# A Mamba-and-ConvLSTM kernel: fold matmuls queued before fills, a later table phase, and paired projection tiles

## The chip, the cores and the metric

The kernel runs on one core of a Trainium2 chip. The time is device microseconds of that core, from one launch; the median of three runs is given. Five engines run their own instruction streams in order and wait for each other through semaphores: TensorE (PE in the profile; PEld is its weight load), VectorE (DVE), ScalarE (ACT), GpSimd (POOL) and SyncE (SP, which issues the DMAs).

## What is computed

The input is `(1, 64, 256, 128)`: 64 channels, T = 256 times, F = 128 frequencies. Layer 0 is a bidirectional Mamba block, first along time (128 sequences of length 256), then along frequency (256 sequences of length 128). Layer 1 is a convolutional LSTM over 32 windows of 8 times. In short:

```python
def _mamba(u, p):
    x, z = split(einsum('nld,ed->nle', u, p['in_proj_w']), 2)
    x = silu(depthwise_conv(x, p['conv_w'], width 4, causal) + p['conv_b'])
    dt, Bm, Cm = split(einsum('nld,ed->nle', x, p['x_proj_w']), [4, 20])
    dt = softplus(dt @ p['dt_proj_w'].T + p['dt_proj_b'])
    def step(h, inp):                       # h: 128 channels x 16 states
        dA = exp(dt_t * A)
        h = dA * h + dt_t * B_t * x_t
        return h, einsum('nds,ns->nd', h, C_t)
    y = scan(step) + x * p['Dp']
    return einsum('nld,od->nlo', y * silu(z), p['out_proj_w'])

def _block(u, p):   return _mamba(_rmsnorm(u, p['norm_w']), p) + u
def _bimamba(u):    return concat([_block(u, pf), flip(_block(flip(u), pb))])
# time stage, then frequency stage:  x = x + _bimamba(x) @ lin_w + lin_b
# layer 1: global norm, unfold, ConvLSTM over 32 windows, transposed conv, prelu, residual
```

All of it is float32.

## The kernel before, in words

`Stage` is run twice, stage 0 along time and stage 1 along frequency. Each cuts its 32,768 positions into 64 chunks of 512. A chunk takes 16 slots: two directions d, two state halves q, four blocks b of 32 channels. Slot S of the loop in `run` handles one (d, q, b) with all 512 positions of two states at once, on tiles of 128 x 1024.

A slot's chain goes over four engines:

- `inputs` ("the fill", line 555): 32 small matmuls of 64 x 32 tiles put dt\*B\*x into one of two `bx` buffers in PSUM. It reads `dtxT` (the transposed dt\*x) and `D` (B spread on a mask by DVE, line 444).
- `decays` (line 575): two ACT exponentials make dA in one of four buffers from `rep`, which a DMA brings from DRAM with each row repeated. Every first use of a buffer in a direction also clears one column (line 572).
- `recur` (line 583): one DVE scan, h = dA\*h + bx, into one of seven `h` buffers (`NH`).
- `outputs` (line 589): POOL multiplies h by `C`, also spread by a DMA.
- every fourth slot, `add_up` ("the fold", line 598): eight matmuls of 128 x 32 tiles add four h tiles into the one bank `y`. Only then are those four h buffers free.

After eight slots DVE's `gate` (line 614) makes `yz` = y\*silu(z); after sixteen, `close_a` and `close_b` (lines 623 to 629) put both directions through the output projection and the residual into `po`, and `keep` (lines 639 and 647) writes X.

The order of the work is written out by hand. In slot S the engines are given: the scan of S, the gate, POOL's product of S-1, the fill of S+2, the decays of S+2, the fold, and then what the table `HEAD` has for this slot. `HEAD` names each preparing step of a chunk with the slot, counted from the start of the chunk before it, at which it is queued. Negative slots lie a further chunk ahead. Each engine runs its share strictly in that order.

The steps of `HEAD` for one chunk, in the order in which data passes through them: `load` u by DMA; `squares`, `means`, `rms` (ACT, TensorE, ACT); `normalise` (POOL writes `xn`, then four DMAs on SP, line 309, copy it into `unp` twice, shifted by one); `project_x` (lines 328 and 329) and `project_z` (line 332) on TensorE, each copied out by ACT to `xs` and `zs`; `silus` (line 353 loads ACT's table, 357); `step_sizes` (pv, line 363); `softplus` (377, 373, and 380 loads the exponential's table again); `project_bc` (line 407, ACT copy line 409, then four DMAs `away<-bc`, line 416); `dt_away` (DMA `there<-dt`, line 386); `times_x` (POOL, line 397); `spread_dt` and `spread_c` (DMAs `rep<-there`, line 459, and `C<-away`, line 453, 512 KB each); `turn` (TensorE transposes, lines 429 and 431, ACT copy 433); `diagonal` (DVE, line 444). "The table phase" is `silus` to `softplus`: three table loads with the silus and the softplus between them, on ACT.

All DMAs stand in SP's one queue, in program order. The tiles `pm`, `px`, `pz`, `pv`, `pb`, `pt` and `po` share two PSUM buffers (`mm`).

Layer 1 (`ConvLstm`, from about 7190 us on) and the start of each stage (`first`) are touched only in that `first` calls the changed helpers.

Of the kernel before, what the change touches and what calls it, by code (L numbers as in the profile page):

```python
# [29 lines left out]
F32 = mybir.dt.float32  # L30
BF16 = mybir.dt.bfloat16
AF = mybir.ActivationFunctionType
# [4 lines left out]
P = 128  # L37
C = 64
T = 256
F = 128  # L40
NS = 16
NBC = 2 * NS
# [3 lines left out]
NU = 4  # L46
W = 64
RANK = 4
NTOK = 512
# [8 lines left out]
FH = F // 2  # L58
HALF = T // 2
NRING = 4  # L60
NREP = 3
RESPOND = 6
NH = 7
LAG = 2
EXP_AND_LN = "natural_log_exp_and_others"
# [5 lines left out]

HEAD = (
    (-13, "load"),
    (-11, "squares"),
    (-6, "means"),
    (-6, "rms"),
    (-5, "normalise"),
    (-2, "project_x", 0),
    (-1, "project_z", 0),
    (-1, "project_z", 1),  # L80
    (0, "project_x", 1),
    (4, "silus"),
    (4, "step_sizes"),
    (5, "softplus"),
    (6, "project_bc", 0),
    (6, "dt_away", 0),
    (6.5, "dt_away", 1),
    (7, "times_x", 0),
    (8.5, "spread_dt", 0, 0),
    (9, "spread_c", 0, 0),  # L90
    (10, "turn", 0),
    (11, "diagonal", 0, 0, 0),
    (12, "spread_dt", 0, 1),
    (12, "project_bc", 1),
    (12.5, "times_x", 1),
    (13, "diagonal", 0, 0, 1),
    (13.5, "spread_c", 0, 1),
    (15, "diagonal", 0, 1, 0),
    (17, "diagonal", 0, 1, 1),
    (17.5, "spread_dt", 1, 0),  # L100
    (17.5, "spread_c", 1, 0),
    (18, "turn", 1),
    (19, "diagonal", 1, 0, 0),
# [3 lines left out]
    (23, "diagonal", 1, 1, 0),  # L107
    (25, "diagonal", 1, 1, 1),
)
SECOND = tuple(x for x in HEAD if x[0] >= 12 and x[1] != "project_bc")  # L110


class Mamba:
# [3 lines left out]
    def __init__(self, ctx, tc, cols, room, d):  # L117
        nc = tc.nc
        self.nc, self.tc, self.d, self.cols = nc, tc, d, cols
        cp = ctx.enter_context(tc.tile_pool(name="m_const", bufs=1))  # L120
# [9 lines left out]
        for i in range(4):  # L130
            for n, t, rows, width in (
                ("g1", self.G1, P, P),
                ("g2", self.G2, P, P),
                ("wz", self.Wz, C, P),
                ("wdt", self.Wdt, P, P),
                ("w2", self.W2, P, C),
            ):
                t.append(cp.tile([rows, width], F32, name=f"{n}{i}", tag=f"{n}{i}"))
        for i in range(2):
            self.W3.append(cp.tile([P, 2, C], F32, name=f"w3{i}", tag=f"w3{i}"))  # L140
        b = cp.tile([C, 2], F32, name="lin_b")
        self.b = b
        self.lin_b = [b[:, i : i + 1] for i in range(2)]

        room = room.rearrange("p t f -> p (t f)")
        at = 0
# [16 lines left out]
        for h in range(2):  # L163
            own = slice(h * C, (h + 1) * C)
# [6 lines left out]
    def load(self, first):  # L171
        dma, d = self.nc.sync.dma_start, self.d
        if first:
            dma(out=self.win[:, 0], in_=d["in_proj"][:, 0])
            dma(out=self.cw[:, 0], in_=d["conv_w"][0].partition_broadcast(C))
            dma(out=self.cols, in_=d["cols"])
            dma(out=self.xdt, in_=d["dt_proj"])
            dma(out=self.Wbc, in_=d["x_proj_bc"])
        else:
            dma(out=self.win[:, 1:4], in_=d["in_proj"][:, 1:4])  # L180
            dma(out=self.cw[:, 1:4], in_=d["conv_w"][1:4].partition_broadcast(C))
            dma(out=self.lin, in_=d["lin_w"])
            dma(out=self.b, in_=d["lin_b"])
            dma(out=self.ow, in_=d["out_proj"])

    def shifts(self, i):
# [15 lines left out]
        self.nc.vector.tensor_copy(self.Wdt[i], ps[:, 0:P])  # L202

    def gates(self, i):
        self.nc.vector.tensor_copy(self.Wz[i], self.win[:, i, P : 2 * P])

    def masks(self):

# [16 lines left out]
class Stage:  # L225
# [102 lines left out]
        nc.tensor.matmul(self.seqs(px), lhsT=m.G1[i], rhs=self.unp[:, :, first : first + L], start=True, stop=False)  # L328
        nc.tensor.matmul(self.seqs(px), lhsT=m.G2[i], rhs=self.unp[:, :, second : second + L], start=False, stop=True)  # L329

    def gated(self, pz, i):
        self.nc.tensor.matmul(  # L332
            self.seqs(pz), lhsT=self.m.Wz[i], rhs=self.unp[0:C, :, 3 : 3 + self.L], start=True, stop=True
        )

    def project_x(self, ch, d):
        i = 2 * self.stage + d
# [3 lines left out]
        self.nc.scalar.activation(xs, px, AF.Identity, bias=self.m.cb[:, i : i + 1])  # L341
        self.at["xs", ch, d] = xs

    def project_z(self, ch, d):
        pz = self.mm("pz")
        self.gated(pz, 2 * self.stage + d)
        zs = self.wk.tile([P, NTOK], F32, name="zs", tag="zs", bufs=5)
        self.nc.scalar.copy(zs, pz)
        self.at["zs", ch, d] = zs

    def silus(self, ch):
        nc = self.nc
# [48 lines left out]
        )  # L401
        self.at["dtx", d] = dtx

    def project_bc(self, ch, d):

        pb = self.mm("pb")[0:NBC]
        self.nc.tensor.matmul(pb, lhsT=self.m.Wbc[:, 2 * self.stage + d], rhs=self.at["xs", ch, d], start=True, stop=True)  # L407
        t = self.wk.tile([NBC, NTOK], F32, name="bc", tag="bc")
        self.nc.scalar.copy(  # L409
            self.in_turns(t, "p (u i c) -> p i u c"), self.in_turns(pb, "p (i u c) -> p i u c")  # L410
        )
        away = self.dram.tile([NS // 2, 2, 2, NTOK // 2], F32, name="away", tag="away")
        for g in range(2):
            rows = self.in_turns(t[NS + NS // 2 * g : NS + NS // 2 * (g + 1)], "p (u i c) -> p i u c")
            for i in range(2):
                self.nc.sync.dma_start(
                    out=away[:, i, g].rearrange("a (u c) -> a u c", u=NU), in_=rows[:, i]
                )
        self.at["bc", d], self.at["away", ch, d] = t, away

    def turn(self, ch, d):

        nc, m = self.nc, self.m
        dtx, bc = self.at["dtx", d], self.at["bc", d]
        pt = self.mm("pt")
        bt = self.ps_bt.tile([P, NU, NS], F32, name="bt", tag="bt")
        for u in range(NU):
            own = slice(P * u, P * (u + 1))
            nc.tensor.transpose(pt[:, own], dtx[:, own], m.ident)  # L429
        for u in range(NU):  # L430
            nc.tensor.transpose(bt[:, u], bc[0:NS, P * u : P * (u + 1)], m.ident[0:NS, 0:NS])  # L431
        t = self.wk.tile([P, NU, P], F32, name="dtxT", tag="dtxT", bufs=2)
        nc.scalar.copy(t.rearrange("p u d -> p (u d)"), pt)  # L433
        self.at["dtxT", ch, d], self.at["bt", ch, d] = t, bt
# [35 lines left out]
    def first(self):  # L470


        nc, m = self.nc, self.m
        s, time = 2 * self.stage, self.time
        banks = [self.ps_bx.tile([P, 2, NTOK], F32, name="bx", tag="bx") for _ in range(2)]
# [14 lines left out]
        x, z = {}, {}  # L490
# [23 lines left out]
            m.gates(1)  # L514
            m.dt(1, self.mm("pw"))
        self.shifted(banks[0][:, 1], s + 1)
        for d in range(2):
            self.gated(banks[1][:, d], s + d)
        nc.scalar.preload_act_table_set(SILU)
        nc.scalar.activation(x[1], banks[0][:, 1], AF.Silu, bias=m.cb[:, s + 1 : s + 2])  # L520
        for d in range(2):
# [94 lines left out]

    def close_a(self, ch):
        nc, m = self.nc, self.m  # L620
        u, w3 = self.at["u", ch], m.W3[self.stage]
        self.po = po = self.mm("po")
        nc.tensor.matmul(po[0:C], lhsT=m.W2[2 * self.stage], rhs=self.at["yz", 0], start=True, stop=False)  # L623
        n = NTOK // 2
        for h in range(2):
            nc.tensor.matmul(po[0:C, h * n : (h + 1) * n], lhsT=w3[:, h], rhs=u, start=False, stop=False)

    def close_b(self, ch):
        self.nc.tensor.matmul(  # L629
            self.po[0:C], lhsT=self.m.W2[2 * self.stage + 1], rhs=self.at["yz", 1], start=False, stop=True  # L630
        )

    def keep(self, ch):
        nc, nseq, po = self.nc, self.nseq, self.po
        bias = self.m.lin_b[self.stage]
        if self.time:
            res = po[0:C].rearrange("p (f h t) -> p h t f", f=nseq, h=2)
            for h in range(2):
                nc.scalar.activation(
                    self.X[h * C : (h + 1) * C, :, ch * nseq : (ch + 1) * nseq], res[:, h], AF.Identity, bias=bias  # L640
                )
        else:
            res = po[0:C].rearrange("p (h r f q) -> p q r h f", h=2, f=FH, q=2)
            rows = slice(ch * nseq // 2, (ch + 1) * nseq // 2)
            for q in range(2):
                own = slice(q * C, (q + 1) * C)
                nc.scalar.activation(  # L647
                    self.X[own, rows, :].rearrange("p r (h f) -> p r h f", h=2),
                    res[:, q],
                    AF.Identity,  # L650
                    bias=bias,
                    accum_out=self.moments.sums[own, ch : ch + 1],
                )

    def spread_of(self, ch):

# [7 lines left out]
    def run(self):  # L664
        nch = NCH
        last = 16 * nch
# [6 lines left out]
        for S in range(int(min(steps)), last + LAG + 4):  # L673
# [3 lines left out]
                self.gate(*self.where(S - 8)[:2])  # L677
            if 0 < S <= last:
                self.outputs(S - 1)
            if 0 <= S + 2 < last:  # L680
                self.inputs(S + 2)

            for ahead in ((2, 3) if S % 16 == silu else () if S % 16 == silu + 1 else (2,)):
                if 0 <= S + ahead < last:
                    self.decays(S + ahead)
            if S % 4 == 1 and 4 < S <= last + LAG:
                self.add_up(S - LAG)
            for f, args in steps.get(S, []):
                f(*args)
            if S % 8 == LAG and 0 < S < last:  # L690
                self.skip(*self.where(S)[:2])
            if S % 16 == LAG and S > 16:
                self.close_a(S // 16 - 1)
            if S % 16 == LAG + 1 and S > 16:
                self.close_b(S // 16 - 1)
                self.keep(S // 16 - 1)
            for f, args in steps.get(S + 0.5, []):
                f(*args)
            if not self.time and S > 16:
# [5 lines left out]
                n = S // 16 - 1  # L705
                if S % 16 == RESPOND:
                    if 0 < n < 21:
# [533 lines left out]
```

## Time and profile before

| what | value |
|---|---|
| time, median of 3 runs | 7876.34 us (7869.36 to 7904.41) |
| the profiled execution: time, span | 7882.31 us, 7880.5 us |
| mean granted TensorE clock | 0.91 of full |
| scans: number, first and last start | 2048, at 46.7 and 7185.4 us |
| busy, share of the span: PE, DVE, ACT, POOL | 81%, 81%, 62%, 71% |
| DMA: moved, mean rate | 695.10 MB, 88 GB/s |

In the profile, a line of a group names the code line, the engine, the operation, output and input tiles with their shapes, the count, and then the busy time, the mean of one in ns, and the idle time of that engine just before with what ended most of it. In a timeline a line has start and length in us. A matmul in float32 shows as two records, so that `px` with its two matmuls is four records. Engines overlap; the shares of busy time are means over the whole span, while a chunk of 16 slots repeats 128 times and takes about 55 us of it.

### The profile page before, as it was taken

To read this page: it belongs to the slowest core of one execution; us is meant where nothing else is said; L and a number is where in the kernel's file an instruction comes from. 1 tells how busy PE (TensorE), PEld (TensorE's weight loads), DVE (VectorE), ACT (ScalarE), POOL (GpSimd) and SP (SyncE) were. 2 spreads that over 40 slices of the span, in tenths; PEclk is the share of its full clock that TensorE was granted. 3 is DMA by queue.
4 is the path that set the end of the run, shared out by engine and by line. 5 is a ranking of instruction groups with operands and counts; after the bars stand their busy time and mean duration, and the time that the engine had idled before them with its cause. 6 is when DMAs were issued, how large, how long until landed. Compare 5 with 4: busy or idle time off the path is not lost.

```text
span 7880.5 us, 324564 instructions
## 1 busy us (share of the span) xinstructions
PE 6410.5 (81%) x148488; PEld 3602.5 (46%) x148488; DVE 6363.7 (81%) x4166; ACT 4921.4 (62%) x8918; POOL 5571.1 (71%) x2898
## 2 busy tenths in 40 slices
PE   7878788888878787877888888877878777877999
PEld 3444444444444444443444444444444444445887
DVE  6888888888888888876888787888878888886887
ACT  6666666666666666665666666666666666664333
POOL 5777777777777777775777777777777777775554
PEclk8889999988899898988999898999889899998999
DMA  2222222222222222222323222222222222221000
GB/s 91 96 94 98 97 97 95 97 95 94 96 95 97 94 98 94 98 92 72 101 98 102 95 100 95 96 94 94 94 91 96 92 98 93 94 96 64 13 16 17
DMA packets 301986, 695.10 MB, mean 88 GB/s; under 512 B 72772, under 2 KB 129732, under 8 KB 300616
## 3 DMA queue, kind: packets, MB, share of 16 engines
q1 hardware_dynamic: 300616, 674.33, 25.3%
q8 instruction: 1166, 19.10, 1.1%
q14 instruction: 204, 1.67, 0.1%
HBM read 557.25 MB, written 83.89 MB: 81 GB/s over the span
## 4 chain that ended last, share of the span: by engine, by line
PE 33%; DVE 9%; ACT 5%; issue 4%; DMA 1%; POOL 1%; SPq 0%; DVEq 0%; POOLq 0%; ACTq 0%
PE bx L555 9%; DVE h L583 7%; PE cv L1003 6%; PE y L598 5%; PE pv L363 3%; ACT dA L575 2%; DVE D L444 2%; PE px L328 2%; PE pz L332 2%; PE px L329 1%; ACT L353 1%; ACT X L647 1%; PE po L629 1%; PE po L623 1%; POOL h L589 1%
## 5 line engine op out<-in xcount | busy, mean ns | idle before, releaser
L589 POOL TENSOR_TENSOR h<-h,C 128x1024 f32<-128x1024 f32 x2048 | 4824.4, 2371 | 1456.4 <-DVE h L583 1324.6
L583 DVE TENSOR_TENSOR_SCAN h<-dA,bx 128x1024 f32<-128x1024 f32 x2048 | 4614.8, 2275 | 1018.8 <-PE y L598 812.6
L555 PE MATMUL bx<-D,dtxT 64*32 64x128 f32 x131072 | 2578.3, 292 | 880.1 <-DVE h L583 872.5
L555 PEld LDWEIGHTS bx<-D,dtxT 64*32 64x32 f32 x131072 | 1994.9, 112 | 2351.7 <-DVE h L583 1007.3
L575 ACT ACTIVATE dA<-rep,cols 128x510 f32<-128x510 f32 (+1 forms) x4096 | 2657.0, 709 | 12.0 <-DVE h L583 6.0
L444 DVE TENSOR_TENSOR D<-mask,bt 128x1024 f32<-128x1024 f32 x1026 | 1226.0, 1195 | 9.7 <-PE bt L431 9.7
L598 PE MATMUL y<-h,fold 128*32 128x512 f32 x8192 | 1085.1, 648 | 6.0 <-POOL h L589 6.0
L363 PE MATMUL pv<-xs,wdt 128*128 128x512 f32 x512 | 452.2, 1035 | 510.3 <-ACT xs L357 508.8
L433 ACT COPY dtxT<-pt 128x512 f32<-128x512 f32 x256 | 150.0, 586 | 966.2 <-PE pt L429 966.1
L341 ACT ACTIVATE xs<-px,cols 128x512 f32<-128x512 f32 x252 | 173.6, 689 | 573.7 <-PE px L329 573.7
L409 ACT COPY bc<-pb 32x512 f32<-32x512 f32 x256 | 147.4, 576 | 518.7 <-PE pb L407 517.6
L598 PEld LDWEIGHTS y<-h,fold 128*32 128x32 f32 x8192 | 229.7, 118 | 520.5 <-issue 504.8
L397 POOL TENSOR_TENSOR dtx<-dt,xs 128x512 f32<-128x512 f32 x256 | 326.9, 1277 | 162.4 <-ACT dt L373 146.9
L363 PEld LDWEIGHTS pv<-xs,wdt 128*128 128x128 f32 x512 | 133.6, 286 | 666.6 <-ACT xs L357 595.9
L614 DVE TENSOR_TENSOR yz<-y,zs 128x512 f32<-128x512 f32 x256 | 176.9, 691 | 291.2 <-PE y L598 291.2
L407 PE MATMUL pb<-xs,wbc 128*32 128x512 f32 x512 | 311.9, 696 | 0.0
L328 PE MATMUL px<-unp,g 128*128 128x512 f32 x504 | 285.5, 648 | 22.1 <-DMA unp<-xn 20.5
L329 PE MATMUL px<-unp,g 128*128 128x512 f32 x504 | 259.1, 595 | 0.0
L332 PE MATMUL pz<-unp,wz 64*128 64x512 f32 x504 | 250.7, 616 | 0.0
L1126 POOL TENSOR_TENSOR y<-v,X 128x512 f32<-128x512 f32 x32 | 40.7, 1271 | 230.5 <-DVE v L1124 230.5
L572 ACT COPY dA<-zeros 128x4 f32<-128x4 f32 (+1 forms) x1024 | 194.9, 190 | 3.3 <-DVE h L583 3.2
L373 ACT ACTIVATE dt<-pv,cols 128x512 f32<-128x512 f32 x256 | 172.5, 687 | 25.3 <-issue 20.5
(191 smaller groups left out, 5458.1 us busy)
## 6 DMA issues: line engine op xcount, KB each, us to landing
rep<-there SPq DMA_DIRECT2D x512, 512.0 KB
C<-away SPq DMA_DIRECT2D x512, 512.0 KB
there<-dt SPq DMA_DIRECT2D x1024, 64.0 KB
unp<-xn SPq DMA_DIRECT2D x504, 64.0 KB
away<-bc SPq DMA_DIRECT2D x1024, 8.0 KB
u<-in_x SPq DMA_DIRECT2D x128, 64.0 KB
out<-y SPq DMA_DIRECT2D x32, 256.0 KB
w<-in_W_ih_f SPq DMA_DIRECT2D x10, 512.0 KB
```

Source lines behind the costliest of these rows:

```text
L328: nc.tensor.matmul(self.seqs(px), lhsT=m.G1[i], rhs=self.unp[:, :, first : first + L], start=True, stop=False)
L329: nc.tensor.matmul(self.seqs(px), lhsT=m.G2[i], rhs=self.unp[:, :, second : second + L], start=False, stop=True)
L332: self.nc.tensor.matmul(self.seqs(pz), lhsT=self.m.Wz[i], rhs=self.unp[0:C, :, 3 : 3 + self.L], start=True, stop=True)
L363: self.nc.tensor.matmul(pv, lhsT=self.m.Wdt[i], rhs=self.at["xs", ch, d], start=True, stop=True)
L397: self.nc.gpsimd.tensor_mul(self.in_turns(dtx, own), self.in_turns(self.at["dt", ch, d], natural), self.in_turns(self.at["xs", ch, d], nat ...
L444: self.nc.vector.tensor_mul(D, self.m.mask.unsqueeze(1).unsqueeze(1).to_broadcast([P, n, 2, W]), b.unsqueeze(3).to_broadcast([P, n, 2, W]),)
L555: self.nc.tensor.matmul(bx[DB * j : DB * (j + 1), i, :, u], lhsT=dtxT[rows, u, DB * b : DB * (b + 1)], rhs=D[rows, u, j], start=True, stop ...
L575: nc.scalar.activation(dA[:, :, g, :, live], rep[:, :, :, live], AF.Exp, scale=m.A[:, k, n : n + 1])
L583: self.nc.vector.tensor_tensor_scan(h[:, step], dA[:, step], bx[:, step], 0.0, ALU.mult, ALU.add)
L589: self.nc.gpsimd.tensor_mul(h, h, self.at["C", ch, d, q])
L598: nc.tensor.matmul(y[DB * b : DB * (b + 1)].rearrange("p (i t) -> p i t", i=2), lhsT=self.m.fold, rhs=hs[b][:, g], start=False, stop=q == ...
L1003: self.nc.tensor.matmul(t[:, g, :, 0:n_out], lhsT=wts[s][:, gate * P : (gate + 1) * P], rhs=self.parts[n][:, :, s : s + n_out], start=s == ...
```

## The change

Five things are done together.

1. In `run`, the fold (`add_up`) of a slot is queued ahead of the fill (`inputs`) and the decays, where it stood behind them.
2. `HEAD` is moved: `silus` and `step_sizes` from slot 4 to 6, `softplus` 5 to 7, `project_bc` of d=0 from 6 to 8, `dt_away` 6 and 6.5 to 8 and 8.5, `times_x` of d=0 7 to 8.5, `spread_dt` 8.5 to 9.5, `spread_c` 9 to 10.5, `squares` 5 to 8.5 (-11 to -7.5). `decays` runs one slot further ahead in the slot that has `silus`, so that dA of the next two slots (now 8 and 9) is queued ahead of the table phase. `RESPOND`, a small step of 20 chunks in stage 1, goes from slot 6 to 12.
3. `project_z` does both directions in one step. The weights of d=1 lie on rows 64 to 127 and are multiplied with the copy of xn on those rows, so that the two matmuls use different halves of TensorE's rows.
4. `project_bc` does both directions in slot 8: two matmuls into different 32-column groups, one ACT copy of 64 partitions, eight `away` DMAs. The step of d=1 in slot 12 is gone.
5. `close_a` and `close_b` become `close`, in slot 3 of the next chunk: each matmul of 512 positions becomes two of 256 that write different halves of `po`'s partitions. The residual's two of 256 become four of 128. `keep` is one ACT instruction over 128 partitions where it was two over 64.

```diff
-RESPOND = 6
+RESPOND = 12
 HEAD = (
-    (-11, "squares"),
+    (-7.5, "squares"),
...
-    (-1, "project_z", 0),
-    (-1, "project_z", 1),
+    (-1, "project_z"),
     (0, "project_x", 1),
-    (4, "silus"),
-    (4, "step_sizes"),
-    (5, "softplus"),
-    (6, "project_bc", 0),
-    (6, "dt_away", 0),
-    (6.5, "dt_away", 1),
-    (7, "times_x", 0),
-    (8.5, "spread_dt", 0, 0),
-    (9, "spread_c", 0, 0),
+    (6, "silus"),
+    (6, "step_sizes"),
+    (7, "softplus"),
+    (8, "project_bc", 0, 1),
+    (8, "dt_away", 0),
+    (8.5, "dt_away", 1),
+    (8.5, "times_x", 0),
+    (9.5, "spread_dt", 0, 0),
     (10, "turn", 0),
+    (10.5, "spread_c", 0, 0),
     (11, "diagonal", 0, 0, 0),
     (12, "spread_dt", 0, 1),
-    (12, "project_bc", 1),
...
-    (17.5, "spread_dt", 1, 0),
+    (17, "spread_dt", 1, 0),
...
+    def gated(self, pz):
+        for d in range(2):
+            rows = slice(d * C, (d + 1) * C)
+            self.nc.tensor.matmul(
+                self.seqs(pz[d]),
+                lhsT=self.m.Wz[self.stage][rows],
+                rhs=self.unp[rows, :, 3 + d : 3 + d + self.L],
+                start=True, stop=True,
+            )
...
+    def project_bc(self, ch, *ds):
+        pb = self.mm("pb")
+        for d in ds:
+            nc.tensor.matmul(pb[NBC * d : NBC * (d + 1)],
+                lhsT=self.m.Wbc[:, 2 * self.stage + d], rhs=self.at["xs", ch, d], start=True, stop=True)
+        bc = self.wk.tile([2 * NBC, NTOK], F32, name="bc", tag="bc")
...
+    def close(self, ch):
+        self.po = self.mm("po")[:, 0 : NTOK // 2]
+        for d in range(2):
+            self.close_by(self.at["yz", d], m.W2[2 * self.stage + d], d)
+            for h in range(2):
+                own = self.po[h * C : (h + 1) * C]
+                if d == 0 and self.time:
+                    n = NTOK // 4
+                    for i in range(2):
+                        nc.tensor.matmul(own[:, i * n : (i + 1) * n], lhsT=w3[:, i],
+                            rhs=u[:, 0, h * n : (h + 1) * n], start=False, stop=False)
...
+    def close_by(self, yz, w2, d):
+        for h in range(2):
+            if self.time:
+                own = yz.rearrange("p (f h t) -> p h f t", f=2, h=2)[:, h]
+                to = self.po[h * C : (h + 1) * C].rearrange("p (f t) -> p f t", f=2)
+            else:
+                own = yz.rearrange("p (n q) -> p q n", q=2)[:, h]
+                to = self.po[h * C : (h + 1) * C]
+            self.nc.tensor.matmul(to, lhsT=w2, rhs=own, start=d == 0, stop=d == 1)
...
     def run(self):
                 self.outputs(S - 1)
+            if S % 4 == 1 and 4 < S <= last + LAG:
+                self.add_up(S - LAG)
             if 0 <= S + 2 < last:
                 self.inputs(S + 2)
             for ahead in ((2, 3) if S % 16 == silu else () if S % 16 == silu + 1 else (2,)):
                 if 0 <= S + ahead < last:
                     self.decays(S + ahead)
-            if S % 4 == 1 and 4 < S <= last + LAG:
-                self.add_up(S - LAG)
...
-            if S % 16 == LAG and S > 16:
-                self.close_a(S // 16 - 1)
             if S % 16 == LAG + 1 and S > 16:
-                self.close_b(S // 16 - 1)
+                self.close(S // 16 - 1)
                 self.keep(S // 16 - 1)
```

In the changed kernel's own numbering the fill is line 570, the fold 613, px 327 and 328, z 333, the first table load 359, B/C's copy 424, the xn DMAs 308.

## The prediction

> **What bounds the kernel now.** I began with the page's groups (line, operation | busy us, mean ns | idle before, releaser): DVE's scan is the costliest work, and what it mostly waits for is a fold.
>
> ```profile
> L583 DVE TENSOR_TENSOR_SCAN h<-dA,bx 128x1024 f32<-128x1024 f32 x2048 | 4614.8, 2275 | 1018.8 <-PE y L598 812.6
> ```
>
> Next the line of the first table load, which runs once per chunk, in each stage. Its first and last starts give the chunk period: (3519.2-68.2)/62 = 55.66 us in stage 0 and (7103.0-3669.5)/62 = 55.38 in stage 1.
>
> ```profile
> L353 ACT ACT_TABLE_LOAD  x63: 1283/1283/1283, 68.2 to 3519.2; - x63
> ...
> L353 ACT ACT_TABLE_LOAD  x63: 1283/1283/1283, 3669.5 to 7103.0; - x63
> ```
>
> DVE alone would need about 45 us: undisturbed scans start 2.2 us apart, 3.3 with a D behind, 2.8 with a yz; 6x2.2 + 8x3.3 + 2x2.8 = 45.2. So 10 us per chunk are stalls. The timeline of one chunk shows the large one (start, length, engine, line):
>
> ```profile
> 1512.12 1.28 ACT L353 ACT_TABLE_LOAD   x1
> ...
> 1514.10 3.46 PE L363 MATMUL pv<-xs,wdt 128*128 128x512 f32 x4 [3.96 <-ACT xs L357]
> ...
> 1517.49 1.32 PE L555 MATMUL bx<-D,dtxT 64*32 64x128 f32 x64
> ...
> 1518.74 1.92 PE L598 MATMUL y<-h,fold 128*32 128x512 f32 x16
> ...
> 1520.79 2.29 DVE L583 TENSOR_TENSOR_SCAN h<-dA,bx 128x1024 f32<-128x1024 f32 x1 [6.45 <-PE y L598]
> ```
>
> TensorE waits 3.96 us for the silus, then pv, the fill and only then the fold that frees the seventh h buffer; the scan of slot 7 pays 6.45 us. Smaller stalls of the same kind (0.9 to 1.4 us) stand at slots 2, 10 and 15.
>
> Then I looked for what comes next, in SP's queue and the DMA windows (us, five engines, PEclk, DMA share of 16 engines, GB/s):
>
> ```profile
> 1473.31 0.52 SPq L459 DMA_DIRECT2D rep<-there  x1
> 1473.87 0.53 SPq L453 DMA_DIRECT2D C<-away  x1
> 1482.22 2.44 SPq L309 DMA_DIRECT2D unp<-xn  x4
> ```
>
> ```profile
> 1483.00:1486.00 3.00, 1.78 (x64) 1.53 (x64) 3.00 (x2) 1.45 (x3) 3.00 (x3) 0.62 0.59 157
> 1486.00:1488.00 2.00, 2.00 (x42) 0.60 (x35) 2.00 (x3) 0.31 (x1) 2.00 (x1) 0.71 0.26 90
> ...
> 1510.00:1519.00 9.00, 5.04 (x83) 2.18 (x76) 4.34 (x3) 8.88 (x13) 7.29 (x4) 0.81 0.26 104
> 1520.00:1524.00 4.00, 3.60 (x137) 1.90 (x130) 3.21 (x2) 2.62 (x8) 0.85 (x1) 1.00 0.02 7
> ```
>
> A rep or C transfer alone keeps a share of 0.26, which is four engines of 16, at 104 GB/s: 524 KB take 5.1 us. The packets bear this out: 4 KB ones run four abreast, 159 ns each. The small xn transfers issued at 1482.22 use all 16 (0.59). Of their 256 packets of 1 KB, 192 pass by 1486; the other 64, on the four busy engines, come only when rep and C are through, the last at 1487.8. So xn lands 14.5 us after rep is issued: in 61 chunks of stage 0 the mean is 14.84 (spread 0.44), in stage 1 15.23, and xn's landing follows rep's issue (correlation 0.8), not its own. px of the next chunk (line 328) needs xn.
>
> **The change part by part.** I count from the first table load, T=0, to the next; the shown chunk has 1455.76 and 1512.12.
>
> *Fold before fill.* Eight fold matmuls take 1.86 us; in the new place they run while the scan of their slot does, for POOL's last product is ready by then (2.37 us, begun with the scan's end). Together with the later table phase (fills 22 to 24 and both dA of slots 24 and 25 are queued ahead of pv), the 6.45 us stall goes, and most of the smaller ones: about 9 of the 10. Cost nil while POOL is on time; a late product would hold the fill, which has 2 us of slack.
>
> *Pairs.* That such tiles run side by side is shown: eight 128*32 folds take 1.86 us, where po alone (128*64, 512 columns, line 629) takes 1.07. So z goes from 1.92 to 0.98, B/C from 2x1.05 to 1.05, po from 2.9 to 1.7 (columns 256 side by side: 0.48 twice, four of 128 partly so: 0.72). Bounds of the pairs together in the chain below: 0 and 2.2 us gained. I take the full gain, being nearest the fold row. The two X writes of 0.485 each become one of 0.5.
>
> *Table phase and B/C later.* This moves the SP chain. Before, B/C's copy (line 409) ends 11.2 us after T, between dA; now it stands behind the phase (7.52 us, 1512.12 to the end of the third load) and dA of slot 26 (1.43): 7.52+1.43+0.6 = 9.6. SP then issues both away sets, four more at 0.33 = +1.33 (they used to come at slot 12), eight there and rep, which from the first away takes 5.9 in the mean. So rep is issued at 9.6+1.33+5.9 = 16.8 (before: 17.4). C and the four xn follow at once, yet on the four engines xn still stands behind rep and C: 16.8+14.8+0.2 = 31.8 for px in stage 0, 32.2 in stage 1.
>
> Before, px starts 33.8 to 36 us after T, so that landing was covered by the stall at slot 7. The cover is now gone: fill 16 ends near T+24, and px stands until 31.8. Behind it in TensorE's queue wait fill 17, z, fill 18, the second px, the fold and fill 19; DVE has no bx for slot 17. The wait is about 7.5 us.
>
> *From px to the next T.* Before 20.5 (1491.61 to 1512.12), paced by TensorE. Now, warm: px 1.92, fill 1.08, z 1.0, fill 1.08, px 1.92, fold 1.86, fill 1.1, so scan 19 starts at +10.2. But TensorE comes from a wait, and the clock column says what that costs:
>
> ```profile
> 1510.20:1514.00 3.80, 0.00 (x0) 0.00 (x0) 3.80 (x3) 3.77 (x7) 3.46 (x2) 1.00 0.27 105
> 1514.10:1517.50 3.40, 3.40 (x5) 0.98 (x6) 0.24 (x1) 3.37 (x5) 2.35 (x1) 0.55 0.25 102
> ```
>
> After 3.8 us without work pv runs at 0.55 of the clock, 3.46 us for two matmuls that px does in 1.92. After 7.5 us px should pay the same 1.5, and the fill behind it 0.3: scan 19 at +12.0. From there: scan 2.28, fill 21 1.2, po 1.7, X 0.5, then four dA pairs (2.56 for two, 2.85 for the two with zeros, newly ahead of the phase): 11.2. Sum 23.2; stage 1 has the dev square (0.4, line 662, in ACT's queue between xs and dA 17): 23.6.
>
> Periods: 31.8+23.2 = 55.0 against 55.66, and 32.2+23.6 = 55.8 against 55.38. 63x(-0.66) + 63x0.42 = -15 us on the profiled 7882.3 (span 7880.5), 7867; that run lies 6 above the median of those shown, so 7862. RESPOND's move (20 small copies) and squares at 8.5, used at slot 10, cost nothing: TensorE and ACT wait there.
>
> The Trainium skill ("DMA: Bandwidth & Descriptors", Anatomy of one DMA) fits a transfer as 2.0 us plus bytes over 436 GB/s, written for the path through GpSimd; the estimate for 512 KB would be 3.2 us rather than the 5.1 of the rows, rep and C would clear some 4 us sooner, and the time would be near 7380. The rows decide; they show four engines, not 16.
>
> **Rivals.**
> (a) *Pairs run one after the other.* Then z keeps 1.92 and po 2.9, and both lie between px and T: +2.2 per chunk, 7862+126x2.2 = 8139. Decided by the start distances of z and po; from +0.43 per chunk, (7916-7862)/126, it counts as slower. For: no 64x128 pair on different row halves is in the trace, and the four 128-column pieces of po are ordered half by half. Against: fills (64*32) run eight abreast.
> (b) *px is not slowed, or xn lands a little sooner:* scan 19 at +10.2, 7862-126x1.7 = 7648. For: the clock windows last 3.41 us and sit at random; now xn is queued early. Against: pv, which always follows such a wait, takes 3.1 to 3.8 us in nine chunks of ten.
> (c) *xn does not stand behind rep and C:* no wait at px, DVE's 45.2 plus about 2 of small stalls: 7876-126x8.3 = 6830. Against: the 64 packets after 1486.
> (d) *The stall at slot 7 stays* (dA or fill still late): period as before, 7876.
>
> **How the numbers follow.** Forecast, the wait moves to px and takes back what the fold frees: 0.46, with its own range 7740 to 7980 (1 us per chunk either way). (a) 0.22, partly or wholly; (b) 0.18; (c) 0.06; (d) 0.08. A measurement of this kernel tells 0.5%, some 39 us, from no change: faster is under 7837, slower over 7916. The forecast splits 0.16/0.14/0.16; (b) and (c) are faster, (a) slower, (d) the same: 0.40, 0.22, 0.38. The range 7640 to 8060 leaves out (c), the far half of (a) and the end of (b), 0.2 in all.
>
> **What would show it.** Right: idle before px (line 327) put down to DMA unp<-xn, about 7 us per chunk, 900 in all; the scan's idle before slot 7 gone and a new one before slot 17; px after it near 1.7 us per matmul with a clock of about 0.5. Pairs: z from first to next fill 1.0, po 1.7. Wrong: px at T+25 with no DMA wait (then (c)), pv's line still followed by a 6 us stall (then (d)), or first away later than T+10.

## The result, and the profile after

The changed kernel takes 7971.94 us (median of 4 runs, 7970.16 to 7979.07), against 7879.31 before (4 runs): the ratio is 1.0114, 95% interval 1.009 to 1.0139. That is slower, where the prediction said 7862, a change too small to be told from none. The profiled execution took 7979.07 us, with a span of 7977.3.

The page's groups (line, operation | busy us, mean ns | idle before, releaser) show the scan's idle time no longer behind a fold but behind dA, and a new group of TensorE with an idle time of over 1000 us. First the changed kernel's lines, then px and pv of the kernel before:

```profile
L598 DVE TENSOR_TENSOR_SCAN h<-dA,bx 128x1024 f32<-128x1024 f32 x2048 | 4615.6, 2276 | 1403.8 <-ACT dA L590 1063.9
...
L327 PE MATMUL px<-unp,g 128*128 128x512 f32 x504 | 399.8, 886 | 1067.3 <-DMA unp<-xn 1067.3
...
L369 PE MATMUL pv<-xs,wdt 128*128 128x512 f32 x512 | 276.9, 666 | 49.0 <-ACT xs L363 47.5
```

```profile
L328 PE MATMUL px<-unp,g 128*128 128x512 f32 x504 | 285.5, 648 | 22.1 <-DMA unp<-xn 20.5
...
L363 PE MATMUL pv<-xs,wdt 128*128 128x512 f32 x512 | 452.2, 1035 | 510.3 <-ACT xs L357 508.8
```

pv, which waited 4 us per chunk before, now waits 0.4 and runs at full speed (666 ns per record, 1035 before). px, which hardly waited, waits 1067/126 = 8.5 us per chunk, for xn. The starts of the first table load give the periods, (3555.7-73.3)/62 = 56.17 us and (7209.6-3694.8)/62 = 56.69, where they were 55.66 and 55.38:

```profile
L359 ACT ACT_TABLE_LOAD  x63: 1283/1283/1283, 73.3 to 3555.7; - x63
...
L359 ACT ACT_TABLE_LOAD  x63: 1283/1283/1283, 3694.8 to 7209.6; - x63
```

The timeline of one chunk, from one table load (T = 1480.14) to the next, is the whole loop (start, length, engine, line, what was done, idle time before and its releaser):

```profile
1478.34 4.46 DVE L598 TENSOR_TENSOR_SCAN h<-dA,bx 128x1024 f32<-128x1024 f32 x2
...
1480.14 1.28 ACT L359 ACT_TABLE_LOAD   x1
...
1482.12 1.98 PE L369 MATMUL pv<-xs,wdt 128*128 128x512 f32 x4 [0.29 <-ACT xs L363]
...
1489.44 2.71 SPq L433 DMA_DIRECT2D away<-bc  x8
...
1496.49 0.53 SPq L475 DMA_DIRECT2D rep<-there  x1
1497.07 0.52 SPq L469 DMA_DIRECT2D C<-away  x1
1497.68 2.43 SPq L308 DMA_DIRECT2D unp<-xn  x4
...
1512.39 2.07 PE L327 MATMUL px<-unp,g 128*128 128x512 f32 x2 [8.01 <-DMA unp<-xn]
...
1514.26 1.92 PE L328 MATMUL px<-unp,g 128*128 128x512 f32 x2
...
1516.10 1.60 PE L570 MATMUL bx<-D,dtxT 64*32 64x128 f32 x64
1516.21 0.69 ACT L346 ACTIVATE xs<-px,cols 128x512 f32<-128x512 f32 x1 [8.84 <-PE px L328]
...
1516.88 1.33 ACT L590 ACTIVATE dA<-rep,cols 128x510 f32<-128x510 f32 x2
...
1517.63 1.13 PE L333 MATMUL pz<-unp,wz 64*128 64x512 f32 x4
1518.30 2.29 DVE L598 TENSOR_TENSOR_SCAN h<-dA,bx 128x1024 f32<-128x1024 f32 x1 [8.55 <-ACT dA L590]
...
1528.28 0.65 PE L671 MATMUL po<-yz,w 128*64 128x256 f32 x4
...
1529.20 0.65 PE L671 MATMUL po<-yz,w 128*64 128x256 f32 x4
...
1535.46 1.28 ACT L359 ACT_TABLE_LOAD   x1
```

The two scans at 1478.34 are those of slots 6 and 7; they run back to back, so the stall of slot 7 is gone. xn is issued by 1500.1, and px starts at 1512.39. The scan of slot 17 stands 8.55 us: ACT's xs copy waits for px, and dA of slot 17 stands behind that copy in ACT's queue. The fill of slot 17, also behind px, ends at 1517.7, half a microsecond before that dA. The clock in windows around this wait (last columns: PEclk, DMA share, GB/s):

```profile
1504.40:1512.30 7.90, 0.00 (x0) 0.00 (x0) 4.34 (x3) 1.33 (x2) 5.65 (x3) 0.66 0.26 97
1512.40:1516.00 3.60, 3.60 (x4) 1.16 (x4) 0.00 (x0) 0.00 (x0) 1.16 (x1) 0.50 0.26 105
```

During the wait the DMA engines keep a share of 0.26, four of 16; then px's two matmuls take 3.7 us at half the clock.

### The profile page after: what moved, and what is told of

Its sections match the earlier page's. It is cut to its first block, busy times and chain, and to the rows that moved or that the text cites. A ratio compares the mean times of both kernels' runs of the same rounds, so it can differ in the third digit from the quotient of the medians.

```text
span 7977.3 us, 325404 instructions
## 1 busy us (share of the span) xinstructions
PE 5895.4 (74%) x149512; PEld 3497.4 (44%) x149512; DVE 6357.9 (80%) x4166; ACT 4741.7 (59%) x8600; POOL 5563.0 (70%) x2898
## 5 line engine op out<-in xcount | busy, mean ns | idle before, releaser
L590 ACT ACTIVATE dA<-rep,cols 128x510 f32<-128x510 f32 (+1 forms) x4096 | 2648.1, 711 | 874.6 <-DMA rep<-there 874.6
L570 PE MATMUL bx<-D,dtxT 64*32 64x128 f32 x131072 | 2418.5, 281 | 900.3 <-DVE h L598 880.8
L570 PEld LDWEIGHTS bx<-D,dtxT 64*32 64x32 f32 x131072 | 1901.4, 108 | 2044.1 <-issue 881.7
L613 PE MATMUL y<-h,fold 128*32 128x512 f32 x8192 | 1212.2, 660 | 5.0 <-POOL h L604 5.0
L327 PE MATMUL px<-unp,g 128*128 128x512 f32 x504 | 399.8, 886 | 1067.3 <-DMA unp<-xn 1067.3
L327 PEld LDWEIGHTS px<-unp,g 128*128 128x128 f32 x504 | 100.3, 249 | 1123.3 <-DMA unp<-xn 903.9
L613 PEld LDWEIGHTS y<-h,fold 128*32 128x32 f32 x8192 | 257.6, 116 | 596.9 <-issue 585.5
L328 PE MATMUL px<-unp,g 128*128 128x512 f32 x504 | 365.9, 819 | 0.0
L369 PE MATMUL pv<-xs,wdt 128*128 128x512 f32 x512 | 276.9, 666 | 49.0 <-ACT xs L363 47.5
L328 PEld LDWEIGHTS px<-unp,g 128*128 128x128 f32 x504 | 132.6, 263 | 190.5 <-issue 190.5
L625 ACT ACTIVATE y<-xs,cols 128x512 f32<-128x512 f32 x256 | 175.6, 686 | 7.0 <-DVE yz L629 7.0
L671 PE MATMUL po<-yz,w 128*64 128x256 f32 x1024 | 170.9, 399 | 0.0
L445 PE MATMUL pt<-ident,dtx 128*128 128x128 f32 x1024 | 168.6, 287 | 0.8 <-POOL dtx L403 0.8
```

Of the source, the lines that this page charges most:

```text
L369: self.nc.tensor.matmul(pv, lhsT=self.m.Wdt[i], rhs=self.at["xs", ch, d], start=True, stop=True)
L570: self.nc.tensor.matmul(bx[DB * j : DB * (j + 1), i, :, u], lhsT=dtxT[rows, u, DB * b : DB * (b + 1)], rhs=D[rows, u, j], start=True, stop ...
L590: nc.scalar.activation(dA[:, :, g, :, live], rep[:, :, :, live], AF.Exp, scale=m.A[:, k, n : n + 1])
L613: nc.tensor.matmul(y[DB * b : DB * (b + 1)].rearrange("p (i t) -> p i t", i=2), lhsT=self.m.fold, rhs=hs[b][:, g], start=False, stop=q == ...
```

## The experiments

All times below are medians, and ratios are to the kernel before in the same batch (7881.5, 7885.3 and 7883.5 us).

**C behind xn.** In the changed kernel, one entry of `HEAD` is moved past the xn DMAs.

```diff
-    (10.5, "spread_c", 0, 0),
     (11, "diagonal", 0, 0, 0),
+    (11.5, "spread_c", 0, 0),
```

> The changed kernel with spread_c of the first quarter (slot 10.5) queued behind the xn DMAs (11.5); nothing else. Theory (xn stands behind rep and C on four DMA engines, and px waits for it): xn now stands behind rep alone and lands about 5.9 us sooner, px starts near T+27 instead of T+33.1. The second rep then comes relatively later and the four engines, busy 45 us of each chunk, are nearly the bound, so not all of it is kept: period about 52.5 against 56.4, time near 7480 (7350 to 7650), and px's idle for DMA unp falls from 8 us to 2 or 3 per chunk. Rival (the wait is xn's own way through SP and its write): px unmoved, 7970.

Measured: 7589.82 us, ratio 0.9627 (0.9606 to 0.9647). From T, px starts at 28.0 in the mean where it was 33.2; the period is 53.4. So one 512 KB transfer ahead of xn is worth 5 us of px's wait. Not all of it is kept, because px to the next T grows from 23.2 to 25.4: ACT now waits more for the later rep transfers, which stand in the same four engines. The waits of this kernel (who for whom: us, times, longest) have it twice per chunk, where the changed kernel has 874.6 us in 134 times:

```profile
ACT dA L590 <- DMA rep<-there: 1252.3, 258, 9.2
```

**rep and C over 16 engines, in the changed kernel and in the one before.** Each transfer is cut into four of 32 partitions.

```diff
-        self.nc.sync.dma_start(out=t, in_=away.unsqueeze(1).to_broadcast([NJ, DB, 2 * NTOK]))
+        for j in range(NJ):
+            self.nc.sync.dma_start(
+                out=t[DB * j : DB * (j + 1)], in_=away[j].unsqueeze(0).to_broadcast([DB, 2 * NTOK])
+            )
...
-        self.nc.sync.dma_start(
-            out=t, in_=there[:, 2 * h : 2 * h + 2].unsqueeze(0).to_broadcast([NJ, DB, 2, NTOK])
-        )
+        for j in range(NJ):
+            self.nc.sync.dma_start(out=t[DB * j : DB * (j + 1)], in_=there[:, 2 * h : 2 * h + 2])
```

> The changed kernel with each rep and C transfer cut into four DMAs of 32 partitions, so that each should use 16 engines instead of four. Theory: rep and C pass in about 3 us instead of 12, xn lands near T+25, no wait at px beyond 2 us, period 47.5 to 49, time 6950 to 7150. SP has 24 DMAs more per chunk, 12 us more of issuing, which is still under the period. Rival (xn's own way): 7970 or, with the extra issuing in SP's chain, 8200.

> The kernel before with the same cut of rep and C. Theory: there px comes when TensorE gets to it (34 us after T), not when xn lands (32), so the period stays: 7880 within 1%. Rival (the four engines bound both kernels): several per cent faster here too.

Measured: the changed kernel 6959.48 us, ratio 0.8823 (0.8801 to 0.8846); the kernel before 7837.95, ratio 0.9953 (0.9933 to 0.9973). A window of the first, in which rep and C pass, has a DMA share of 0.96 at 232 GB/s:

```profile
1530.00:1538.00 8.00, 7.92 (x148) 3.71 (x152) 6.22 (x5) 5.17 (x12) 5.89 (x3) 1.00 0.96 232
```

The same edit is worth 0.5% where the stall of slot 7 covers xn's landing, and 12.7% (6959/7972) where that stall is gone. In the kernel before, xn's last packet comes 2.7 us sooner with the cut (29.7 us after T, 32.4 without) and px does not move (34.8 and 34.9). In the changed kernel px moves from 33.2 to 26.7 us after T. That is most of the 8 us that each chunk gains; the rest lies behind px, which the shorter wait (2.1 us) slows less: 2.4 us from its start to the next fill, where it was 3.65. This is the sharpest evidence for the mechanism: the four engines are not the bound of the kernel before, and they are the bound of px in the changed one.

**Matmuls that keep TensorE busy while px waits.** Six matmuls of 128x512 on the identity, ahead of px, into px's own tile, which px's first matmul overwrites.

```diff
+        if d == 0:
+            for _ in range(WARM):
+                self.nc.tensor.matmul(px.rearrange("p (a b) -> p a b", a=4), lhsT=self.m.ident,
+                    rhs=self.m.ident.unsqueeze(1).to_broadcast([P, 4, P]), start=True, stop=True)
```

> The changed kernel with six matmuls of 128x512 on the identity ahead of the first px, into px's own tile, which px then overwrites; they fill TensorE's wait. Theory: px and the fill behind it run at full clock, px to the next T falls from 23.1 to about 21.3, period -1.8, time near 7745 (7680 to 7830). Rival (the half clock is covered by something else): 7970, or more if the six last beyond xn's landing.

Measured: 7920.39 us, ratio 1.0039 (1.0019 to 1.0059): 52 us under the changed kernel, where 225 were expected. The expectation was missed. In the chunk shown the six ended early, and px was slow all the same after a 2.76 us wait:

```profile
1498.43 1.95 PE L328 MATMUL px<-unp,g 128*128 128x512 f32 x2 [2.76 <-DMA unp<-xn]
1500.18 1.91 PE L329 MATMUL px<-unp,g 128*128 128x512 f32 x2
```

So the test was too weak, and it was repeated with nine.

> As a_warm, with nine matmuls of 128x512 instead of six, because six ended 2.8 us before xn landed and px was slow again in the chunk looked at. Theory (px pays the half clock, 1.8 us per chunk): px's matmuls fall from 0.9 us busy per record to about 0.6, time near 7750 (7700 to 7830). Rival: as a_warm, 7920, or 7970 and more if nine run past the landing.

Measured: 7771.31 us, ratio 0.9854 (0.9828 to 0.988), 201 us under the changed kernel. px's records fall to a mean of 649 ns with little idle left, and px to the next T is 21.3 us where it was 23.2, as expected:

```profile
L328 PE MATMUL px<-unp,g 128*128 128x512 f32 x504 | 286.1, 649 | 145.0 <-DMA unp<-xn 144.7
```

The half clock after the wait costs 1.6 (201/126) to 1.9 us (23.2 - 21.3) per chunk, more than the whole loss of the change, 0.7.

**The pairs undone.** z on rows 0 to 63 for both directions, po in 64 partitions of 512 columns and two X writes, as in the kernel before; the rest as changed.

```diff
-                lhsT=self.m.Wz[self.stage][rows],
-                rhs=self.unp[rows, :, 3 + d : 3 + d + self.L],
+                lhsT=self.m.Wz[2 * self.stage + d],
+                rhs=self.unp[0:C, :, 3 : 3 + self.L],
...
-                self.close(S // 16 - 1)
+                self.close_a(S // 16 - 1)
+                self.close_b(S // 16 - 1)
```

> The changed kernel with z and po as before the change: both z matmuls on rows 0 to 63, po in 64 partitions of 512, two X writes, all of po in slot 3; the paired B/C stays. Theory (z, po and X lie in the chain from px to the next T): z +0.9, po +1.35, X +0.5 = +2.7 us per chunk, time near 8310 (8200 to 8400). Rival (pairs are no gain, or cost a change of tiling): 7970 or less.

Measured: 8304.43 us, ratio 1.0535 (1.0508 to 1.0563). px to the next T is 25.8 us, 2.6 more than with the pairs. In the changed kernel z takes 1.06 us from its first matmul to the next fill, and po 1.60 in the whole; here they take 1.93 and 2.79 (medians). So the pairs do run side by side, and their gain falls on the loop: without them the change would cost 5%.

**The fold's place alone**, in the kernel before.

```diff
+            if S % 4 == 1 and 4 < S <= last + LAG:
+                self.add_up(S - LAG)
             if 0 <= S + 2 < last:
                 self.inputs(S + 2)
...
-            if S % 4 == 1 and 4 < S <= last + LAG:
-                self.add_up(S - LAG)
```

> The kernel before with the fold ahead of the fill and nothing else. Theory: the stall of slot 7 stays, since pv is queued ahead of both; the smaller stalls at slots 2, 10 and 15 go, so px moves up from 34.4 to 36 us after T until it meets xn's landing plus 1.0 (33.2): 1 to 2 us per chunk, time near 7700 (7630 to 7830). Rival (the fold's place gives the whole gain): 7500 or less.

Measured: 7763.26 us, ratio 0.9843 (0.9823 to 0.9862). In this kernel's groups the scan waits for a fill instead of a fold, and no less (1018.8 before). What has gone is the wait of yz, which reads what the folds have added up; its line of the kernel before stands last:

```profile
L583 DVE TENSOR_TENSOR_SCAN h<-dA,bx 128x1024 f32<-128x1024 f32 x2048 | 4619.8, 2276 | 1191.7 <-PE bx L555 1058.1
...
L614 DVE TENSOR_TENSOR yz<-y,zs 128x512 f32<-128x512 f32 x256 | 170.6, 666 | 13.9 <-PE y L598 13.7
```

```profile
L614 DVE TENSOR_TENSOR yz<-y,zs 128x512 f32<-128x512 f32 x256 | 176.9, 691 | 291.2 <-PE y L598 291.2
```

The interval between the scans of slots 6 and 7 even grew, from 8.9 to 9.6 us, since the fill now stands behind the fold; the gain comes from slot 2 (3.9 to 3.1 from its scan to the next) and slot 10 (4.2 to 2.8), where the gate stands (stage 0).

**The table phase put back**, with the fold first, the pairs and one B/C as changed.

```diff
-    (6, "silus"),
-    (6, "step_sizes"),
-    (7, "softplus"),
-    (8, "project_bc", 0, 1),
+    (4, "silus"),
+    (4, "step_sizes"),
+    (5, "softplus"),
+    (6, "project_bc", 0, 1),
```

and `dt_away`, `times_x`, the first rep and C, `squares` and `RESPOND` at their old slots.

> The changed kernel (fold first, pairs, one paired B/C) with the slots of HEAD put back: silus 4, softplus 5, B/C of both directions and dt_away 6, times_x 7, rep and C 8.5 and 9, squares -11, RESPOND 6. Theory: the stall of slot 7 comes back and covers xn again, px starts near 34.6 with TensorE warm, the four dA no longer stand ahead of the table load (two do), px to T is about 18.5: period about 53, time near 7570 (7480 to 7680). So the later phase alone turns a gain of 4% into the loss of 1%. Rival (the stall's removal is worth its price, the loss is from the pairs or the fold): 7970 or more.

Measured: 7672.79 us, ratio 0.9736 (0.9717 to 0.9755). px starts 35.0 us after T and the rest takes 18.9; T lies two slots earlier in the chunk here, so only the sum compares with the changed kernel (53.9 and 56.4). The stall of slot 7 is back (8.2 to 8.5 us between the scans of slots 6 and 7), and the kernel is nevertheless 299 us faster than the changed one. Of the five parts, the later phase, with the steps of `HEAD` that move with it, is the one that turns the gain into a loss.

**The fold first, with rep and C cut.** The edit of the fold's place and the edit of the two transfers together, in the kernel before, as they stand above.

> b_fold with rep and C cut into four DMAs each. Theory: xn is out of the way, what is left is the stall of slot 7 and TensorE's own work up to px: period 52.5 to 54, time 7500 to 7680, against 7763 without the cut. So without the later phase the same cut is worth 1 to 3%, with it 12%. Rival (the cut helps whatever the order): 6960 to 7100.

Measured: 7749.37 us, ratio 0.9837 (0.9821 to 0.9853). The time expected was missed: the cut is worth 14 us, not 80 to 260. I had taken xn's landing for the limit of the kernel with the fold first, but px waits for xn only 40 us in all there:

```profile
L328 PE MATMUL px<-unp,g 128*128 128x512 f32 x504 | 285.0, 647 | 40.4 <-DMA unp<-xn 40.0
```

With the cut it is 8.3 us, xn's last packet comes 3.3 us sooner, and px moves by 0.1 (34.2 and 34.1 us after T). So TensorE's own queue, in which pv waits for the silus (553.8 us in all), sets px there. What the two theories differed in stands: without the later phase the cut brings nearly nothing.

**A version that beats both.** The changed kernel with the cut transfers and the first C behind xn: those two edits together, as they stand above.

> a_lanes with C of the first quarter queued behind the xn DMAs. Theory: what is left of px's wait there (about 2 us per chunk) falls by C's share, some 2 us of issuing and 1.5 us of transfer; the period goes from 48.5 to about 47, time near 6800 (6720 to 6900). Rival (DVE is the bound already): 6960.

Measured: 6696.0 us, ratio 0.849 (0.8473 to 0.8507), under the range expected. px's wait for xn falls from 267.7 us with the cut alone to 26.8, and px starts 24.6 us after T instead of 26.7. DVE is busy 95% of the span and the scan's idle time has fallen to a ninth of the changed kernel's:

```profile
PE 5612.8 (84%) x149512; PEld 3384.9 (51%) x149512; DVE 6336.0 (95%) x4166; ACT 4742.8 (71%) x8600; POOL 5563.0 (83%) x2898
...
L600 DVE TENSOR_TENSOR_SCAN h<-dA,bx 128x1024 f32<-128x1024 f32 x2048 | 4602.4, 2273 | 149.2 <-PE bx L572 78.7
```

Its periods are 45.9 and 46.7 us, against the 45.2 that DVE alone needs. With the transfers out of the way the whole change takes 9 us per chunk off the 55.7 and 55.4 of the kernel before, nearly all of the 10 that stood as stalls. No run shows how much of this the pairs bring.

## Why the prediction was right or wrong

The mechanism held in the main: the wait moved to px, for the reason given. The direction was missed by the size of the terms up to px, one of them above all. The loop as predicted, and as the changed kernel's trace has it (means over the chunks of stage 0 / stage 1, us):

| term | predicted | measured |
|---|---|---|
| T to rep's issue | 16.8 / 16.8 | 16.9 / 17.05 |
| rep's issue to xn's last packet | 14.8 / 15.2 | 15.2 / 15.3 |
| last packet to px | 0.2 / 0.2 | 1.03 / 1.0 |
| px to the next T | 23.2 / 23.6 | 23.1 / 23.3 |
| period | 55.0 / 55.8 | 56.2 / 56.7 |

The step that failed is "16.8+14.8+0.2 = 31.8 for px". The 0.2 was a guess for what lies between the last packet of xn and the start of px, and 0.8 us too small; the transfer before it was 0.1 to 0.4 too short, rep's issue 0.1 to 0.25 too early, and px to T 0.1 to 0.3 too long. In sum the periods are 1.16 and 0.89 us longer, times 63 chunks each: 129 us on 7867 give 7996, where 7979 was measured; the rest lies mostly outside the periods (between the stages and behind the last T the changed kernel is 21 us shorter, ahead of the first T 5 longer). The 0.2 alone makes up some 100 of the 129 us, more than the whole change measured. The gap shows in the packets of the chunk above. The last of xn's 1 KB packets starts at 1511.18. Of the two stretches to 1511.3 and from there on, the first has 84 packets under 2 KB (64 of xn's, and 20 under 512 B) and the second none, while px starts at 1512.39:

```profile
DMA packets 122, 0.22 MB, mean 96 GB/s; under 512 B 20, under 2 KB 84, under 8 KB 122
```

```profile
DMA packets 21, 0.09 MB, mean 78 GB/s; under 512 B 0, under 2 KB 0, under 8 KB 21
```

The number could have been read from the trace of before: px waited for xn there nine times (20.5 us), with a gap between last packet and px of 0.8 to 1.2 us in seven of them, and of 0.5 in the two at the start of a stage. The Trainium skill ("DMA: Bandwidth & Descriptors", Anatomy of one DMA, written for the path through GpSimd) says that a completion is signalled only when the last byte is confirmed in the target memory, and puts most of 2 us on that; the 1.0 here, into SBUF, is half of it.

That px to the next T came out within 0.3 us is partly luck. The pieces that the prediction lists add up to 9.96 and 11.09 where it writes 10.2 and 11.2; by them the forecast would have been some 40 us lower still. The path between them was told wrongly, too: the prediction counts TensorE's queue up to the scan of slot 19. In the trace (stage 0) DVE stands at slot 17 for dA, behind ACT's xs copy, and not for bx; that scan starts 5.9 us after px, and from there DVE's own pace takes 6.6 us to the scan of slot 19. So that scan comes 12.5 us after px, not 12.0, and the way from there to T takes 10.6, not 11.2.

Point by point:

- *The stall at slot 7 goes* (its cover gone, px exposed): right. 2.2 us lie between the scans of slots 6 and 7, the floor, and 10.7 to 11.0 between those of slots 0 and 1 (slots 16 and 17 above). Rival (d) falls.
- *xn stands behind rep and C on four engines*: right, shown by the cut in both kernels and by C behind xn. Rival (c) falls. It was priced at 6830 for a kernel in which px does not wait; with the cut 6959 was measured, where px still waits 2.1 us per chunk, and with C behind xn as well 6696, where it waits 0.2. The fit of the skill's page, by which the time came to 7380, divides by 436 GB/s, where four engines moved 104 here; the same page (Why a DMA increments its semaphore by 16 and not by 1) says that a transfer is split over the largest number up to 16 that divides the slowest dimension of both sides. That is 4 for the uncut rep and 16 for the cut one, and the shares 0.26 and 0.96 agree.
- *px pays the half clock, 1.5 and 0.3 with the fill*: right, shown by nine matmuls in the wait, and somewhat too small: 3.65 us from px to the fill (1.93 before) and 1.52 for the fill (1.09). Rival (b) falls in both halves, since xn also landed later and not sooner.
- *Pairs at full gain*: right. 2.6 us per chunk against the 2.2 and 0.5 of X that were counted; rival (a) falls.
- *Fold before fill, about 9 of 10 us of stalls*: right for the DVE side together with the later phase, as the periods of 45.9 and 46.7 us show. Alone it brings 1.6%, and nothing at slot 7, as pv stands ahead of both in TensorE's queue.

What stayed open: whether the blocked DMA issues described below cost anything of their own, and what makes an issue block.

## What to carry to other kernels

A stall that is removed uncovers the next arrival on the same loop, and its price is then set by terms that cost nothing before, here to less than a microsecond: take the time from a transfer's last packet to its reader from waits that the trace already has, and don't leave it to a guess. Read a transfer's width from the DMA share (0.26 of 16 engines is four) before an order of issues is trusted: the small xn transfers, issued behind two narrow ones, landed only after them. When the sum of a loop comes out within 1% of the old period, the sign is not known, and the better question is which term can be taken out of the loop.

## What was not expected of the hardware

Issuing a DMA can itself block. In the changed kernel SP's issue of C took 507 ns at least, 553 in the middle and 7952 at most, that of rep 6327 at most (before: 3016 and 734). Of the 512 issues of C 243 took over 1.5 us, where 2 did before. And in the chunk above the C issued at 1500.88, the fourth of the large transfers queued since 1496.49, holds SP for 4.74 us:

```profile
1500.88 4.74 SPq L469 DMA_DIRECT2D C<-away  x1
```

A short wait, too, can cost TensorE its clock. In the kernel with six matmuls px ran at half speed behind a wait of 2.8 us (1.95 and 1.91 us per matmul). Over that kernel's chunks, px took over 3 us to the next fill (1.9 at full speed) behind none of the 7 waits under 1.5 us, behind 16 of the 35 from 1.5 to 3 us, behind 45 of the 51 from 3 to 4 us, and behind 30 of the 32 longer ones.
